# An AdaLN block on one core: FFN over pairs of steps, hidden weights read from DRAM, and a fixed plan of issue

## The chip, the cores and the metric

The kernel runs on one core of one Trainium2 chip. The metric is device time in microseconds (us) for one launch. The engines named are TensorE (matmuls; its weight loads are a row of their own in the profile), VectorE, ScalarE (ACT), GpSimd (POOL) and SyncE (SP), whose queue issues nearly all DMAs.

## The reference

An input x of 4 batches x 2048 tokens x 256 channels goes through a memory attention and then through an FFN, each behind a modulated layer norm. Cut to what is computed:

```python
h = layernorm(x) * (1 + ca) + sa          # ca, sa, ga, cb, sb, gb: per batch, from silu(c) @ wmod
x = x + ga * attn(h)
h = layernorm(x) * (1 + cb) + sb
x = x + gb * ffn(h)

# attn: 4 heads of 64, chunks of 64 tokens; rk = h / |h| per head, wk = rk shifted by one token, v = h @ Ww.T
A     = inv(eye - A0)                     # A0 = -(wk wk^T * decay), strictly lower, 64 x 64 per chunk and head
intra = strict(rk wk^T * decay)
def step(S, ...):                         # chunk after chunk
    v_new = A @ v - (A @ wk) @ S
    o     = rk_g @ S + intra @ v_new
    S     = gamma_C * S + wk_g @ v_new
attn = h + (alpha * o) @ Wr.T

# ffn: weights are -1, 0, 1 with a scale per output
h = silu(h @ w1) * (h @ w2)               # 256 -> 1024
h = gelu(h @ h1); h = gelu(h @ h2)        # 1024 -> 1024, erf form
ffn = h @ w3                              # 1024 -> 256
```

## The kernel before

*Steps.* A step is one chunk of 64 tokens of all four batches: 256 rows, held as 128 partitions x 2 halves. There are NS = 32 steps, and each has a local part (norms, keys, values, Gram matrices, the inverse), a recurrent part that needs the state S of the step before, and an FFN.

*Local part.* `local_norms` makes the modulated layer norm `hid` and the unit keys `rk`. `local_keys` transposes both on TensorE (`tp`) into `hT` and `keys`, `local_values` multiplies by Ww (`vp`), and `local_grams` makes the Gram matrices (`G`), masked by VectorE into `NMT` (for A) and `IT` (for intra). The diagonal 32 x 32 blocks go through DRAM (`d1`) into `U`, with one block a partition, 32 of them in four copies. `local_inverse` (L269, L271) inverts all of them by columns: 31 columns, two VectorE operations each, on `Z`. `local_blocks` brings them back over DRAM (`d2`) into `E`, `local_diagonal` transposes them, and `local_merge1` and `local_merge2` compute the off-diagonal blocks (`yp`, `ep`).

*Recurrent part.* `rec_state` multiplies S by the keys (`R`, `O`), `rec_values` multiplies by the inverse (`V`, then `vn`), `rec_update` makes the inner output and the new S (`new`, first the output, then the state), and `rec_out` multiplies by Wr (`ap_`, `ga`) and lets POOL add it to the step's `y` (L393).

*FFN.* `ffn_norm` normalises `y` into `xn`. `ffn_turn` transposes it (`tpf`), ACT applies the modulation in eight operations (`hm`), and `split` (L396 to L399) writes it as a high part, rounded to fp32r, and the low rest, so that two fp32r passes give the product. Eight tiles of `gated` (for w1 and w2, two products of 2 x 2 matmuls each), 16 of `hidden` (8 x 2 matmuls) and two of `last` (16 matmuls) follow. Their matmuls are at L462 in `product`. A tile's ACT or VectorE output is split as the next layer's input, by POOL in `gated` and by VectorE in `hidden`. A matmul of `gated` and `hidden` has 256 columns, the rows of one step. All five FFN weights stay in SBUF. A second branch, `steps(False)`, handles weights that fp32r can't hold; a flag from a comparison in the setup chooses, and with these inputs the first branch runs.

*Order.* `steps` interleaves by hand: while the FFN of step s runs, step s + 1 gets its merges and its recurrent part, step s + 2 its keys, Gram matrices and inverse, and step s + 3 its norms. Its core:

```python
f.gated(0) ... f.gated(7)             # local_keys(s + 2) after gated(1)
local_grams(s + 2); local_merge1(s + 1)
for q in range(16):
    # q 2 merge2, 3 rec_values, 5 rec_update, 7 rec_out, 8 local_values(s + 2),
    # q 9 ffn_norm, 11 ffn_turn(s + 1), 12 local_norms(s + 3)
    f.hidden(q // 8, q % 8)           # two columns of local_inverse(s + 2) after each from q = 3
rec_state(s + 2); f.last(0); f.last(1)
```

`tc.issue_after(x)` holds what is issued inside it behind instruction x; among what is free, a scheduler with a model of the times picks the order on each engine, and each engine then runs its instructions in that order. PSUM has three banks for FFN tiles (`pf`), two double ones for local work (`a2`) and one (`a1`). The local buffers `keys`, `v`, `rkg`, `hid` and `E` exist once, `rk`, `wkg`, `IT` and `NMT` twice, `y` four times.

Of the kernel before, what the change touches and what calls it, by code (L numbers as in the profile page):

```python
# [27 lines left out]
BF = mybir.dt.bfloat16  # L28
I32 = mybir.dt.int32
# [36 lines left out]

@with_exitstack
def adaln_block_kernel(ctx: ExitStack, tc: tile.TileContext, x_in, ww, wr, decay, log_alpha, w1, w2, h1, h2, w3, scol,
# [7 lines left out]
    N = B * C  # L76
    EPS = 1e-5

# [24 lines left out]
    fh1 = cp.tile([P, NH, HID], FR, name="fh1")  # L103
    fh2 = cp.tile([P, NH, HID], FR, name="fh2")
# [4 lines left out]
    ys = [cp.tile([P, 2, D], F32, name=f"y{n}") for n in range(4)]  # L109
    rks = [cp.tile([P, 2, D], F32, name=f"rk{n}") for n in range(2)]  # L110
    keys = cp.tile([P, 2, 2, 2, C + 1], F32, name="keys")
    v = cp.tile([P, 2, D], F32, name="v")
    rem = cp.tile([P, 2, D], F32, name="rem")
    rkg = cp.tile([P, 2, 2, 2, C], F32, name="rkg")
    hid = cp.tile([P, 2, D], F32, name="hid")
    wkgs = [cp.tile([P, 2, D], F32, name=f"wkg{n}") for n in range(2)]
    ITs = [cp.tile([P, 8, C], F32, name=f"IT{n}") for n in range(2)]
    NMTs = [cp.tile([P, 8, C], F32, name=f"NMT{n}") for n in range(2)]
    E = cp.tile([P, 8, C], F32, name="E")
    S = cp.tile([P, 2, 4, C], F32, name="S")  # L120
    U = cp.tile([P, K, K], F32, name="U")
    Z = cp.tile([P, 8, K], F32, name="Z")
    Dm = cp.tile([P, 8, K], F32, name="Dm")
    d1 = dp.tile([4, 8, K, K], F32, name="d1")
    d2 = dp.tile([K, 4, 8, K], F32, name="d2")

    nc.vector.memset(half, -0.5)
    nc.gpsimd.memset(keys, 0.0)
    nc.gpsimd.memset(S, 0.0)
    nc.gpsimd.memset(E, 0.0)  # L130
    nc.gpsimd.memset(wkgs[0], 0.0)
# [4 lines left out]
    mark = {}  # L136

    def after(name):

        return tc.issue_after(mark[name])  # L140

    def move(out, in_):
        mark["moved"] = nc.sync.dma_start(out=out, in_=in_).ins  # L143

    def flat(t):
        return t.rearrange("q n d -> q (n d)")
# [4 lines left out]
    def load(s):  # L151
        for b in range(2):
            move(out=ys[s % 4][C * b:C * b + C],
                              in_=x_in[b::2, s * C:(s + 1) * C, :].rearrange("q t d -> t q d"))

    def moments(x):

        mv = st.tile([P, 2, 2], F32, tag="mv", name="mv")
        for n in range(2):
            bs = st.tile([P, 6], F32, tag="bs", name="bs")  # L160
            nc.vector.bn_stats(bs, x[:, n, :])  # L161
            nc.vector.bn_aggr(mv[:, n, :], bs)
        rs = st.tile([P, 2], F32, tag="rs", name="rs")
        nc.vector.tensor_scalar(rs, mv[:, :, 1], EPS, None, ALU.add)  # L164
        nc.gpsimd.tensor_tensor(rs, rs, half[:, 0:2], ALU.pow)  # L165
        return mv, rs


    def local_norms(s):
        x, rk = ys[s % 4], rks[s % 2]  # L170
        mv, rs = moments(x)
        for n in range(2):
            nc.vector.scalar_tensor_tensor(hid[:, n, :], x[:, n, :], mv[:, n, 0:1], mod[:, CA, n, :],  # L173
                                           ALU.subtract, ALU.mult)
            nc.vector.scalar_tensor_tensor(hid[:, n, :], hid[:, n, :], rs[:, n:n + 1], mod[:, SA, n, :],  # L175
                                           ALU.mult, ALU.add)
        sq = ap.tile([P, 2, D], F32, tag="tmp", name="sq")
        nc.scalar.activation(sq, hid, AF.Square)
        rn = st.tile([P, 8], F32, tag="rn", name="rn")
        nc.vector.tensor_reduce(rn, heads(sq), AX.X, ALU.add)  # L180
        mark["norms"] = nc.vector.tensor_scalar(rn, rn, 1e-24, None, ALU.max).ins  # L181
        nc.gpsimd.tensor_tensor(rn, rn, half, ALU.pow)
        nc.gpsimd.tensor_tensor(heads(rk), heads(hid), over(rn, 2, C), ALU.mult)

    def local_residual(s, h=None):
        x, h = ys[s % 4], hid if h is None else h

        t = ap.tile([P, 2, D], F32, tag="tmp", name="gh")
        nc.gpsimd.tensor_tensor(t, h, mod[:, GA], ALU.mult)  # L189
        nc.gpsimd.tensor_tensor(x, x, t, ALU.add)  # L190

    def local_keys(s, first=False):
        rk = rks[s % 2]
        tp = ps2.tile([P, 2, 2, 2, P], F32, tag="a2", name="tp")
        for a, src in enumerate((hid, rk)):
            for p in range(2):
                for n in range(2):
                    nc.tensor.transpose(tp[:, a, p, n, :], src[:, n, p * P:(p + 1) * P], ident)  # L198
        hT = ap.tile([P, 2, 2, P], F32, tag="hT", name="hT")

        nc.scalar.copy(hT[:, :, 0, :], tp[:, 0, :, 0, :])
        nc.scalar.copy(hT[:, :, 1, :].rearrange("q p (b t) -> q p b t", t=C)[:, :, ::-1, :],
                       tp[:, 0, :, 1, :].rearrange("q p (b t) -> q p b t", t=C))
        k4 = keys.rearrange("q p n b t -> q (p n b) t")
        if s > 0:
            nc.vector.tensor_copy(k4[:, :, 0:1], k4[:, :, C:C + 1])
        nc.scalar.copy(k4[:, :, 1:C + 1], tp[:, 1].rearrange("q p n (b t) -> q (p n b) t", t=C))
        if not first:
            local_residual(s)
        return hT  # L210

    def local_reads():

        nc.gpsimd.tensor_tensor(rkg.rearrange("q p n b t -> q p (n b) t"),
                                keys.rearrange("q p n b t -> q p (n b) t")[:, :, :, 1:C + 1], over(gpT, 2, 4), ALU.mult)

    def local_writes(s):

        rk, wkg = rks[s % 2], wkgs[s % 2]
        for b in range(2):  # L220
            if s > 0:
                move(out=wkg[C * b:C * b + 1], in_=rks[(s - 1) % 2][C * b + C - 1:C * b + C])
            move(out=wkg[C * b + 1:C * b + C], in_=rk[C * b:C * b + C - 1])
        w4 = wkg.rearrange("q n (a d) -> q n a d", d=C)
        mark["keys"] = nc.gpsimd.tensor_tensor(w4, w4, over(over(gtail, 1, 2), 3, C), ALU.mult).ins  # L225

    def local_values(s, hT):
        vp = ps1.tile([P, 2, D], F32, tag="a1", name="vp")
        for n in range(2):
            for k in range(NK):  # L230
                nc.tensor.matmul(vp[:, n, :], lhsT=hT[:, k, n, :], rhs=wwT[:, k, :], start=k == 0, stop=k == NK - 1)  # L231
        nc.scalar.copy(v, vp)

    def local_keys_values(s):
        local_values(s, local_keys(s))

    def local_grams(s):
        IT, NMT = ITs[s % 2], NMTs[s % 2]

        G = ps2.tile([P, 2, 2, 256], F32, tag="a2", name="G")  # L240
        for p in range(2):
            for n in range(2):
                for h in range(2):
                    r = slice(C * h, C * h + C)
                    for b in range(2):
                        mark["grams"] = nc.tensor.matmul(G[C * b:C * b + C, h, p, n * (C + 1):(n + 1) * (C + 1)],
                                         lhsT=keys[r, p, n, b, 0:C], rhs=keys[r, p, n, b, :], start=True, stop=True).ins
        g4 = G.rearrange("q h p m -> q (h p) m")[:, :, 0:2 * (C + 1)].rearrange("q a (n t) -> q a n t", t=C + 1)
        nc.vector.tensor_tensor(NMT.rearrange("q (a n) t -> q a n t", n=2), g4[:, :, :, 0:C], over(NLT, 2, 2), ALU.mult)
        mark["masked"] = nc.vector.tensor_tensor(IT.rearrange("q (a n) t -> q a n t", n=2), g4[:, :, :, 1:C + 1], over(LT, 2, 2),  # L250
                                ALU.mult).ins
        for b in range(2):
            for k in range(2):
                r = slice(C * b + K * k, C * b + K * k + K)
                move(out=d1[2 * b + k].rearrange("u j i -> j u i"), in_=NMT[r, :, K * k:K * k + K])
        for g in range(4):
            move(out=U[K * g:K * g + K], in_=d1.rearrange("x u j i -> (x u) j i"))

        nc.gpsimd.memset(Z, 0.0)  # L259
        diag = Z.rearrange("q c i -> q (c i)")  # L260
        for g in range(4):
            nc.gpsimd.memset(diag[K * g:K * g + K, g::K + 4], 1.0)

    def local_inverse(s, j0, j1):

        for j in range(j0, j1):
            n, w = j // 4 + 1, K - 1 - j
            t = ap.tile([P, 8, K], F32, tag="zt", name="zt")
            nc.vector.tensor_tensor(t[:, 0:n, 0:w], Z[:, 0:n, j:j + 1].to_broadcast([P, n, w]),  # L269
                                    over(U[:, j, j + 1:K], 1, n), ALU.mult)  # L270
            mark["inverse"] = nc.vector.tensor_tensor(Z[:, 0:n, j + 1:K], Z[:, 0:n, j + 1:K], t[:, 0:n, 0:w],  # L271
                                                      ALU.add).ins

    def local_blocks(s):
        dst = d2.rearrange("(c g) x u i -> g (x u) c i", g=4)
        for g in range(4):
            move(out=dst[g], in_=Z[K * g:K * g + K])
        E4 = E.rearrange("q (a n) i -> q a n i", n=2)
        for b in range(2):
            for k in range(2):  # L280
                for n in range(2):
                    r = slice(C * (b ^ n) + K * k, C * (b ^ n) + K * k + K)
                    move(out=E4[r, :, n, K * k:K * k + K],
                         in_=d2[:, 2 * b + k].rearrange("j (a n) i -> j a n i", n=2)[:, :, n, :])

    def local_diagonal():

        E4, D4 = (t.rearrange("q (a n) i -> q a n i", n=2) for t in (E, Dm))
        nc.vector.transpose(D4[:, :, 0, :], E4[:, :, 0, 0:K])
# [515 lines left out]
```

## Time and profile before

| | us |
|---|---|
| median of 3 runs | 1799.43 (1796.76 to 1800.52) |
| profiled execution | 1796.47 |
| its span, first to last instruction | 1794.6 |
| first FFN matmul of step 0 | 96.7 |
| of step 1 | 167.9 |
| of step 2 | 229.07 |
| of step 31 | 1744.5 |
| last FFN matmul ends | 1788.4 |

The four starts are read from the timeline of TensorE. The profile gives, for each engine, its busy share of the span and how many instructions it ran; below it come rows of 40 slices (a digit is the busy share in tenths, PEclk the granted TensorE clock in tenths of full speed), and then groups of instructions as `out<-in` with their count, `busy, mean ns`, and the idle time before them with what ended most of it. Matmuls overlap in the pipe, so the distance between their starts, from the timeline, is the pace, and the mean of one is its latency. The timeline lists time, length, engine, instruction and count, with the idle time and its releaser in brackets. L numbers are lines of the kernel.

### The profile page before, as it was taken

How to read it: one execution, taken by the hardware profiler on the slowest of the kernel's cores; microseconds unless marked ns; L12 is line 12 of the kernel's file. 1: busy time of each engine (PE TensorE's matmuls, PEld its weight loads, DVE VectorE, ACT ScalarE, POOL GpSimd, SP SyncE). 2: the span in 40 equal slices, each digit the busy share in tenths (PEclk: the TensorE clock that was granted, in tenths of full speed). 3: DMA queues.
4: the chain of work that ended last, by engine and by line, in shares of the span. 5: the costliest groups of instructions: out<-in, count | busy, mean ns of one | idle time of the engine just before them, and what ended most of it. 6: DMA issues, size and time to landing. Idle time of an engine off the chain costs nothing.

```text
span 1794.6 us, 50335 instructions
## 1 busy us (share of the span) xinstructions
PE 1704.1 (95%) x20372; PEld 1623.5 (90%) x20372; DVE 1207.6 (67%) x3805; ACT 991.4 (55%) x2285; POOL 595.3 (33%) x742
## 2 busy tenths in 40 slices
PE   5478999999999999999999999999999999999998
PEld 3267999999999999999999999999999999999998
DVE  6876666677766667776666777666777766667532
ACT  5244555655555565555566555556555655665554
POOL 2232323342332334233234323323433333343111
PEclk8688999999999999999999999999999999999999
DMA  8220111111111110111111011111111111110100
GB/s 288 76 52 8 34 40 40 40 21 33 36 32 40 40 40 16 37 35 34 40 40 40 16 37 34 34 40 40 28 25 38 36 34 40 40 38 16 27 7 15
DMA packets 144659, 72.11 MB, mean 40 GB/s; under 512 B 114400, under 2 KB 132960, under 8 KB 144416
## 3 DMA queue, kind: packets, MB, share of 16 engines
q1 hardware_dynamic: 144416, 68.79, 15.6%
q8 instruction: 162, 2.65, 0.6%
q14 instruction: 81, 0.66, 0.1%
HBM read 43.57 MB, written 16.78 MB: 34 GB/s over the span
## 4 chain that ended last, share of the span: by engine, by line
DVE 47%; PE 29%; DMA 9%; POOL 4%; SPq 4%; issue 4%; ACT 2%; DVEq 0%; ACTq 0%; POOLq 0%
PE ps L462 24%; DVE zt L269 14%; DVE Z L271 11%; DVE act L399 6%; DMA out_dram<-y 4%; SPq L143 4%; DMA U<-d 4%; POOL act L399 3%; DVE bs L161 2%; DVE rn L181 2%; POOL y L501 1%; PE tp L198 1%; DVE hid L173 1%; DVE rn L180 1%; DVE hid L175 1%
## 5 line engine op out<-in xcount | busy, mean ns | idle before, releaser
L462 PE MATMUL ps<-act,fh 128*128 128x256 f32 x8192 | 1026.3, 283 | 1.2 <-DVE act L399 0.7
L462 PEld LDWEIGHTS ps<-act,fh 128*128 128x128 f32 x8192 | 981.9, 188 | 11.8 <-DVE act L399 1.2
L481 ACT ACTIVATE raw<-ps,sc 128x256 f32<-128x256 f32 x512 | 244.4, 479 | 407.6 <-PE ps L462 357.4
L269 DVE TENSOR_TENSOR zt<-Z,U 128x60 f32<-128x60 f32 (+24 forms) x992 | 291.7, 294 | 138.6 <-DMA U<-d 107.9
L399 DVE TENSOR_TENSOR act<-raw,act 128x256 fp32r<-128x256 f32 x512 | 213.2, 421 | 212.1 <-ACT act L398 211.9
L398 ACT CAST act<-raw 128x256 fp32r<-128x256 f32 x768 | 311.9, 407 | 39.6 <-DVE raw L473 23.1
L462 PE MATMUL ps<-hs,fw 128*128 128x256 f32 x2048 | 258.5, 283 | 15.6 <-DVE hs L399 6.7
L462 PEld LDWEIGHTS ps<-hs,fw 128*128 128x128 f32 x2048 | 247.9, 190 | 17.5 <-DVE hs L399 7.2
L271 DVE TENSOR_TENSOR Z<-Z,zt 128x60 f32<-128x60 f32 (+24 forms) x992 | 241.1, 243 | 22.2 <-DVE zt L269 0.5
L399 POOL TENSOR_TENSOR act<-raw,act 128x256 fp32r<-128x256 f32 x256 | 187.7, 739 | 148.0 <-ACT act L398 144.5
L393 POOL TENSOR_TENSOR y<-y,ga 128x512 f32<-128x512 f32 x32 | 41.3, 1291 | 503.1 <-DVE ga L392 478.6
L473 DVE SCALAR_TENSOR_TENSOR raw<-ps,sc,sg 128x256 f32<-128x256 f32 x256 | 123.5, 484 | 124.3 <-ACT sg L472 121.1
L472 ACT ACTIVATE sg<-ps,sc 128x256 f32<-128x256 f32 x256 | 122.0, 477 | 152.4 <-PE ps L462 144.0
L462 PE MATMUL ps<-fw,act 128*128 128x256 f32 x1024 | 138.4, 285 | 22.7 <-DVE act L399 22.0
L462 PEld LDWEIGHTS ps<-fw,act 128*128 128x128 f32 x1024 | 123.2, 188 | 33.2 <-DVE act L399 30.2
L165 POOL TENSOR_TENSOR rs<-rs,half 128x2 f32<-128x2 f32 x64 | 53.9, 842 | 132.3 <-DVE rs L164 132.3
L417 ACT ACTIVATE hm<-tpf,modT 128x64 f32<-128x64 f32 x256 | 82.3, 416 | 13.1 <-PE tpf L413 13.0
L231 PE MATMUL vp<-wwT,hT 128*128 128x256 f32 x256 | 63.8, 394 | 14.8 <-DVE modT L667 14.8
L189 POOL TENSOR_TENSOR gh<-hid,mod 128x512 f32<-128x512 f32 x32 | 50.8, 1586 | 75.4 <-DVE rn L180 75.3
L225 POOL TENSOR_TENSOR wkg<-wkg,gtail 128x512 f32<-128x512 f32 x32 | 33.4, 1042 | 115.9 <-DMA wkg<-rk 42.2
L231 PEld LDWEIGHTS vp<-wwT,hT 128*128 128x128 f32 x256 | 48.2, 198 | 21.0 <-ACT alc L645 15.2
L259 POOL MEMSET Z<- 128x256 f32 x32 | 10.1, 317 | 161.8 <-DMA d<-Z 161.8
(213 smaller groups left out, 1565.0 us busy)
## 6 DMA issues: line engine op xcount, KB each, us to landing
U<-d SPq DMA_DIRECT2D x128, 128.0 KB, 2.7
y<-in_x_dram SPq DMA_DIRECT2D x64, 128.0 KB, 2.9
st<-in_h_dram SPq DMA_DIRECT2D x16, 512.0 KB, 6.2
wkg<-rk SPq DMA_DIRECT2D x64, 126.0 KB
out_dram<-y SPq DMA_DIRECT2D x62, 128.0 KB, 2.5
d<-NMT SPq DMA_DIRECT2D x128, 32.0 KB, 1.6
d<-Z SPq DMA_DIRECT2D x128, 32.0 KB, 1.7
E<-d SPq DMA_DIRECT2D x256, 16.0 KB, 1.7
```

What stands on the lines that cost most here:

```text
L143: mark["moved"] = nc.sync.dma_start(out=out, in_=in_).ins
L165: nc.gpsimd.tensor_tensor(rs, rs, half[:, 0:2], ALU.pow)
L231: nc.tensor.matmul(vp[:, n, :], lhsT=hT[:, k, n, :], rhs=wwT[:, k, :], start=k == 0, stop=k == NK - 1)
L269: nc.vector.tensor_tensor(t[:, 0:n, 0:w], Z[:, 0:n, j:j + 1].to_broadcast([P, n, w]), over(U[:, j, j + 1:K], 1, n), ALU.mult)
L271: mark["inverse"] = nc.vector.tensor_tensor(Z[:, 0:n, j + 1:K], Z[:, 0:n, j + 1:K], t[:, 0:n, 0:w], ALU.add).ins
L398: nc.scalar.copy(to[0], a)
L399: return (eng or nc.vector).tensor_tensor(to[1], a, to[0].bitcast(F32), ALU.subtract).ins
L417: nc.scalar.activation(hm[:, k, b, :], tp[:, k, b // 2, C * (b % 2):C * (b % 2) + C], AF.Identity, bias=modT[:, k, b:b + 1], scale=modT[:, ...
L462: self.end = nc.tensor.matmul(ps, lhsT=wk if lhs_is_w else a, rhs=a if lhs_is_w else wk, start=k == 0 and i == 0, stop=k == k_n - 1 and i ...
L472: nc.scalar.activation(sg, ps[:, 0, :], AF.Silu, scale=sc[:, 0, o:o + 1])
L473: self.gate = nc.vector.scalar_tensor_tensor(to, ps[:, 1, :], sc[:, 1, o:o + 1], sg, ALU.mult, ALU.mult).ins
L481: nc.scalar.activation(to, ps[:, 0, :], AF.Gelu, scale=sc[:, 2 + layer, o:o + 1])
```

## The change

The FFN takes two steps at a time: steps 0 and 1 singly, then the 15 pairs 2g and 2g + 1. A matmul of `gated` and `hidden` then has up to 512 columns (N = 2 * B * C), the activations of a pair are one tile, and `last` still runs 128 rows a matmul, four times. In `gated` each of the two products has a PSUM bank of its own. POOL makes the low part for the first six gated tiles, VectorE for the last two.

The hidden weights no longer stay in SBUF. The setup writes h1 and h2 to DRAM, reordered so that what one output tile needs (512 KB) is contiguous, and each hidden tile reads its own into a ring of three. The setup's comparison with a rounded copy is replaced by a look at the low 16 bits of each weight. The SBUF that comes free holds second copies of `keys`, `v` and `rkg`, six `y`, and IT, E, Z, Dm for two steps; E takes the place of NMT and `rem` is gone.

The Gram matrices, the inverse and the merges are made for two steps at once: U holds 64 blocks twice instead of 32 blocks four times, one a partition, and Z 16 instead of 8 of their columns a partition. In `rec_update` the state's matmuls and the update of S come before the inner output.

The order of issue is a list. An FFN is cut into units (`yield`), 84 in a single FFN and 88 in a pair, and every local or recurrent function is put at a unit by `planned`; `stage` holds it behind the last instruction of every engine so far. `later` counts half as many units during the two single FFNs.

```diff
-    N = B * C
+    NP = NS // 2
+    N = 2 * B * C
+    def stage():
+        with ExitStack() as stack:
+            for e in engines:
+                if e.last is not None:
+                    stack.enter_context(tc.issue_after(e.last))
+            yield
...
-    fh1 = cp.tile([P, NH, HID], FR, name="fh1")
-    fh2 = cp.tile([P, NH, HID], FR, name="fh2")
+    fhs = [dp.tile([NH, P, NH, P], F32, name=f"fh{n}") for n in range(2)]
...
-    def local_inverse(s, j0, j1):
-        for j in range(j0, j1):
-            n, w = j // 4 + 1, K - 1 - j
+    def local_inverse(j):
+        n, w = j // 2 + 1, K - 1 - j
+        t = ap.tile([P, 16, K], F32, tag="zt", name="zt")
+        dve.tensor_tensor(t[:, 0:n, 0:w], Z[:, 0:n, j:j + 1].to_broadcast([P, n, w]), over(U[:, j, j + 1:K], 1, n),
+                          ALU.mult)
+        dve.tensor_tensor(Z[:, 0:n, j + 1:K], Z[:, 0:n, j + 1:K], t[:, 0:n, 0:w], ALU.add)
...
+        GATED, GELU, LAST = 16, 64, 8
+        UNITS = GATED + GELU + LAST
...
         def hidden(self, layer, o):
-            w, src = ((fh1, h1), (fh2, h2))[layer]
-            ps = pf.tile([P, 2, N], F32, tag="f", name="ps2")
-            self.product(ps[:, 0, :], self.weights(w, src, o * P, P))
+            ps = pf.tile([P, self.n], F32, tag="f", name="ps2")
+            if self.exact:
+                w = self.ring(NH)
+                move(out=w.bitcast(F32), in_=fhs[layer][o])
+            yield from self.product(ps, w, 4)
...
+        def layer(n):
+            to, w, k = parts[n]
+            move(out=to[:, :, k, :].rearrange("o p c -> p o c"), in_=staged[n].rearrange("q (o c) -> q o c", c=P))
...
+    FIRST = 2 * NU - Ffn.LAST
+        def recur(s, u):
+            add(u, rec_values, s, to="vn")
+            add(later(u, 3), rec_update, s, "=vn", "=oT", to="oT")
+            add(later(u, 6), rec_out, s, "=oT")
+            add(later(u, 10), ffn_norm, s, to="xn")
+            add(later(u, 13), turned, s)
+        def local(s, u, new=True):
+            if new:
+                add(u, local_hidden, s, hid, to="sq")
+                add(later(u, 3), local_sizes, "=sq", to="rn")
+                add(later(u, 4), local_units, s, hid, "=rn")
+                add(later(u, 9), local_residual, s, hid)
+            add(later(u, 7), local_shift, s)
+            add(later(u, 8), local_keys, s, hid, to="hT")
+            add(later(u, 11), local_values, s, "=hT")
+            add(later(u, 11), local_reads, s)
+            add(later(u, 12), local_writes, s)
...
+        for g in range(1, NP):
+            a, b = 2 * g, 2 * g + 1
+            if g > 1:
+                u = later(merge, 6)
+                add(max(u - 18, 0), load, a)
+                add(max(u + 2, 0), load, b)
+                local(a, u)
+                u = later(u, 11)
+            local(b, u)
+            add(later(u, 12), local_grams)
+            u = later(u, 21)
+            for j in range(K - 1):
+                add(later(u, j // 2 if g == 1 else j * 2 // 3), local_inverse, j)
+            u = later(u, K // 2 if g == 1 else (K - 2) * 2 // 3 + 1)
+            add(u, local_blocks)
+            merge = max(later(u, 11), FIRST + NU * (g - 2) + 10)
+            m = merge
+            add(m - 4, rec_state, a, to="oT")
+            add(m - 1, local_diagonal)
+            add(m, local_merge1, to="Y")
+            add(later(m, 3), local_merge2, "=Y")
+            recur(a, later(m, 6))
+            add(later(m, 12), rec_state, b, to="oT")
+            recur(b, later(m, 16))
...
+            for g, i in [(0, 0), (0, 1)] + [(g, None) for g in range(1, NP)]:
+                before, f = f, Ffn(g, i, had["hs"], fp, exact)
+                for n, _ in enumerate(f.run()):
...
+                    for what in plan.pop(u, ()):
+                        with stage():
+                            what()
+                    u += 1
```

## The prediction

> **What bounds the kernel now.** I read the page first: busy shares and the row of the granted TensorE clock, then the costliest groups.
>
> ```profile
> span 1794.6 us, 50335 instructions
> PE 1704.1 (95%) x20372; PEld 1623.5 (90%) x20372; DVE 1207.6 (67%) x3805; ACT 991.4 (55%) x2285; POOL 595.3 (33%) x742
> PEclk8688999999999999999999999999999999999999
> L462 PE MATMUL ps<-act,fh 128*128 128x256 f32 x8192 | 1026.3, 283 | 1.2 <-DVE act L399 0.7
> ```
>
> TensorE is full from slice 5 on, its clock is full there, and its 8192 hidden-layer matmuls lose 1.2 us to waits. The 283 ns is latency; what counts is the distance between starts. That is in the timeline of TensorE, over one step in the middle and then over the last step, which has no attention work beside it (columns: start, us, what, count, idle before):
>
> ```profile
> 882.39 0.69 PE L366 MATMUL new<-IT,vn 64*64 64x64 f32 x32
> 882.90 0.65 PE L369 MATMUL new<-vn,wkg 64*64 64x64 f32 x32
> 883.48 3.68 PE L462 MATMUL ps<-act,fh 128*128 128x256 f32 x29
> 887.00 1.89 PE L389 MATMUL ap__13449<-wrT,oT 128*128 128x256 f32 x8
> 888.54 3.53 PE L462 MATMUL ps<-act,fh 128*128 128x256 f32 x27
> 891.91 1.89 PE L231 MATMUL vp<-wwT,hT 128*128 128x256 f32 x8
> ...
> 898.00 0.60 PE L413 MATMUL tpf<-kept,xn 128*128 128x128 f32 x4
> 898.35 9.67 PE L462 MATMUL ps<-act,fh 128*128 128x256 f32 x80
> ...
> 911.12 0.50 PE L462 MATMUL ps<-fw,act 128*128 128x256 f32 x2 [0.33 <-DVE act L399]
> 912.39 2.21 PE L462 MATMUL ps<-fw,act 128*128 128x256 f32 x17 [0.77 <-DVE act L399]
> ```
>
> ```profile
> 1753.53 30.25 PE L462 MATMUL ps<-act,fh 128*128 128x256 f32 x256
> ```
>
> 256 matmuls in 30.25 us, less one latency of 0.28, is 0.1175 us a matmul of 256 columns. The local work of a step costs TensorE, start to next start in that timeline: `new` 1.09, `ap_` 1.54, `vp` 1.54, `tpf` 0.35, R and O 1.09, `tp` 0.79, G 0.63, `yp` 0.38, `ep` 0.62, V 0.63 (those not shown are in the same answer), together 8.66. The 352 FFN matmuls of a step are 41.1 at the mixed pace (256 x 0.1175, 64 gated at 0.113, 32 last at 0.117). Steps repeat every 52.3 us ((1744.5 - 229.07)/29 between the first FFN matmuls of step 2 and of step 31), so 2.5 us a step is waiting: 5.0 in a pair of 104.5.
>
> Where a turn of activations (`tpf`, then `hs`) is not covered, it looks like this, at the start of the second step:
>
> ```profile
> 163.48 0.49 PE L413 MATMUL tpf<-kept,xn 128*128 128x128 f32 x3
> ...
> 167.91 0.80 PE L462 MATMUL ps<-hs,fw 128*128 128x256 f32 x2 [3.82 <-ACT hs L398]
> 171.72 3.23 PE L462 MATMUL ps<-hs,fw 128*128 128x256 f32 x14 [3.02 <-DVE hs L399]
> ```
>
> In the steady steps `tpf` has 80 and more matmuls behind it (898.35), and the turn costs nothing. Last, what the groups say of the parts on other engines:
>
> ```profile
> L269 DVE TENSOR_TENSOR zt<-Z,U 128x31 f32<-128x31 f32 x32 | 6.1, 191 | 113.3 <-DMA U<-d 107.9 <-DMA E<-d 5.4
> L399 DVE TENSOR_TENSOR hs<-hm,hs 128x512 fp32r<-128x512 f32 x32 | 21.9, 684 | 2.4 <-ACT hs L398 2.4
> L398 ACT CAST hs<-hm 128x512 fp32r<-128x512 f32 x32 | 21.2, 661 | 0.1
> U<-d SPq DMA_DIRECT2D x128, 128.0 KB, 2.7
> ```
>
> The first column of the inverse holds VectorE 107.9 us in all (3.4 a step) until U has landed. It costs nothing now, since TensorE is then in the hidden layers.
>
> **What the Trainium skill says.** "TensorE: Matmul & The Clock Gate", Back-to-back issue gap: columns / 2.4 + 2.5 ns, so 109 ns at 256 and 216 at 512. The trace agrees at 512 columns' worth: `vp` takes (1.89 - 0.38)/7 = 0.216 us a pass. It disagrees at 256 (117.5). The section LDWEIGHTS gives columns / 1.2, 107 ns for 128, near the 117.5, and PEld is 90% busy: I read the pace at 256 as that of the weight load. Part 1 of the page lets the clock fall to half after some 3.4 us with little work; the PEclk row has 6 in the third slice, where TensorE had waits of 3 to 15 us. "SBUF — State Buffer", Who interferes with whom: a two-input VectorE operation locks out GpSimd or waits for it; the trace has `zt` of 28 columns at 1.04 us (909.25) beside the usual 0.2.
>
> **The change, part by part.**
>
> *Wider matmuls.* 320 gated and hidden matmuls a pair have 512 columns in place of 640 with 256; the 64 of `last` stay. Cost: 320 x 0.216 + 64 x 0.117 = 76.6 us a pair. Before: 82.2. The bounds are 0.216 (weight load hidden) and 0.235 (no gain, 82.7); I take 0.216 because `vp` with full weights shows it. Local TensorE work is the same, 17.3 a pair. Together 93.9.
>
> *Inverse of two steps at once.* One run of 31 columns for two steps. A pair of operations costs about 0.19 + 0.19 at 31 elements and 0.23 + 0.23 at 70; with up to 136 elements I estimate 0.25 each, 15.5 us against 2 x 31 x 0.41 = 25 now. Off the path: VectorE is at 67%. No credit. ACT and VectorE evictions of 512 columns (0.66 to 0.75 by the rows above, against 0.41 to 0.48) lie beside 3.5 us of matmuls a tile in the hidden layers: nothing.
>
> *Streamed hidden weights.* 16 x 512 KB a pair, one each 3.46 us (151 GB/s). The first slice moved 288 GB/s, and a 128 KB load lands in 2.7 us; at three buffers a slot has 7 us. In the built order of SyncE's queue the loads stand behind transfers that wait for the inverse and for E's blocks, but each has a tile to spare. I take 0; if that cover goes, about 2 us a pair.
>
> *The order of issue, which decides.* In the built order the inverse sits in the gated phase and the first hidden layer, the merges at the start of the second, both recurrences after that, and the second step's turn directly before the next pair's first matmul. Walking the four queues by hand with the durations above:
> 1. At the pair's border the chain runs `ap_`, `ga`, POOL's y, statistics, `xn`, `tpf`, with little FFN work left between. Waits: `tp` for `rk` 0.8 (POOL's two norm operations, 1.66 and 1.06, in front), `vp` for `hT` 0.65, `tpf` for `xn` 1.6.
> 2. After `tpf`, eight `hm` (2.45) and the cast (0.66) come before the first matmul, and G fills 1.26: 2.15 of waiting, then 0.25 for the low half. Items 1 and 2: 5.5.
> 3. Gated phase. VectorE has the masks of two steps and `gb` (5 x 0.68) ahead of the first gate; then the first inverse column stands between the third and the fourth gate and waits for U: masks, d writes, U's landing end 13 us after `tpf`. The fourth gate ends near 17.7, and a matmul needing its bank has waited 2.7. The order of ACT (two Silus, two casts) costs the rest. The phase takes 19.6 against 14.9 of work: 4.7.
> 4. Of the 5.0 waiting before I keep half, 2.5 (layer changes, the port lock, the clock after the border).
>
> Sum 12.7; a pair takes 106.6. Bounds of this sum: 7 (the gated phase costs 1, the chain at the border is 2 shorter, 1 of item 4) to 17 (half clock after each border, late weights).
>
> *Start.* Sixteen 512 KB writes of the reordered weights go out on SyncE's queue before the first blocks: 8.4 MB at 288 GB/s is 29 us after the 45 of loads, so the merges can begin at about 78, not 70.2: +8. Step 1's turn moves into the first FFN: -7 (the 3.82 and 3.02 above). Two single FFNs at 1.9 us a tile need 276 GB/s: +5. The border before the first pair: +5.5. The first two FFNs took 67 and 61 us against 52; of that excess I take 8 back. First pair at 229 + 3.5, say 232.
>
> *Sum.* 232 + 14 x 106.6 + last FFN 79.6 (76.6 and 3 waiting) + tail 6.2 (as now) = 1810 of span; the execution is 1.9 above its span (1796.5 to 1794.6), and the median shown 3.0 above that: 1815.
>
> **Rivals.**
> - *Faster (0.40): the wider matmuls carry.* Waits of 7.7 a pair: 101.6, so 232 + 1422 + 86 = 1740 and 1745 as a median. For: the walk adds every hop, and in the gated phase a shorter way to U removes most of item 3. Against: `tpf` and `hs` stand side by side, and the start of step 2 showed what that costs. It decides from 11.6 us of waiting a pair down; above, the kernel is slower.
> - *Much slower (0.12): the clock falls at every border, and weights come late.* The border leaves TensorE mostly idle for over 6 us. 110 a pair: 1863.
> - *The width gives nothing (0.04):* pace 0.235, 6.1 a pair more: about 1900.
> - *No difference (0.06):* 1796 to 1803; 0.2% is what this measurement can tell.
>
> **How the numbers follow.** The likeliest, slightly slower by the waits at the border and in the gated phase, has 0.38 and its own range 1803 to 1845. Slower in all is 0.38 + 0.12 + 0.04 = 0.54. The range of 1730 to 1863 leaves out the upper half of the last cases and the best fifth of the faster one.
>
> **What would show it.** `vp` and the 512-column matmuls at 0.216 apart: the first part right. A wait of `ps` for ACT's `hs` near 2 us once a pair: item 2. Waits of `ps` in the gated phase for VectorE with `zt` held by U: item 3. A PEclk row with eights would speak for the third case. I am wrong if the pair's period is 102 or less, or if the gated phase takes under 16 us.

## The result and the profile after

The change makes the kernel slower: 1958.62 us (median of 4 runs, 1957.06 to 1963.25) against 1799.68 for the kernel before, a ratio of 1.089 (95% interval 1.087 to 1.091). The prediction was 1815 with a range of 1730 to 1863. The page of the kernel after, profiled in an execution of 1957.66 us:

```profile
span 1955.8 us, 37975 instructions
PE 1731.8 (89%) x15572; PEld 1405.4 (72%) x15572; DVE 1023.3 (52%) x2426; ACT 813.8 (42%) x1467; POOL 509.2 (26%) x474
PEclk7679899999999999999899999999999898999999
```

TensorE has fallen from 95% to 89%, and its clock row, all nines from the fifth slice on before, has eights again and again. Nearly all instructions now show as L82, the line of a wrapper, so tiles identify them. The merges of one pair, then the border to the next, in the timeline of TensorE (start, us, what, count, idle time before and its releaser):

```profile
882.94 0.80 PE L82 MATMUL yp<-Dm,E 32*32 32x32 f32 x64
...
931.12 1.79 PE L82 MATMUL ps<-fw,act 128*128 128x256 f32 x12
932.74 0.60 PE L82 MATMUL tp<-kept,rk 128*128 128x128 f32 x4
933.80 1.99 PE L82 MATMUL vp<-wwT,hT 128*128 128x256 f32 x8 [0.46 <-ACT hT L82]
937.39 0.30 PE L82 MATMUL tpf<-kept,xn 128*128 128x128 f32 x1 [1.59 <-DVE xn L82]
938.64 0.76 PE L82 MATMUL tpf<-kept,xn 128*128 128x128 f32 x3 [0.95 <-DVE xn L82]
939.33 2.01 PE L82 MATMUL G<-keys 64*64 64x65 f32 x64
942.63 8.34 PE L82 MATMUL ps<-hs,fw 128*128 128x512 f32 x28 [1.28 <-ACT hs L82]
...
957.47 2.83 PE L82 MATMUL ps<-hs,fw 128*128 128x512 f32 x8 [2.42 <-DVE raw L82]
960.57 4.95 PE L82 MATMUL ps<-hs,fw 128*128 128x512 f32 x16 [0.27 <-DVE raw L82]
965.62 11.22 PE L82 MATMUL ps<-act,w 128*128 128x512 f32 x48
978.75 2.87 PE L82 MATMUL ps<-act,w 128*128 128x512 f32 x8 [1.92 <-DMA w<-fh]
```

These are the places that the prediction walked: `xn`, `hs`, then the gates (`raw`) behind the inverse. The last of these is seen on VectorE, where the first column of the inverse stands between the third gate (950.18) and the fourth (956.67) and waits for U:

```profile
953.85 0.19 DVE L82 TENSOR_TENSOR zt<-Z,U 128x31 f32<-128x31 f32 x1 [2.92 <-DMA U<-d]
```

But 28 matmuls take 8.34 us at 942.63, where 28 at 0.227 (the pace at 965.62, (11.22 - 0.43)/47 = 0.230, hardly differs) take 6.8. The table of stretches says why (stretch, length, busy time of TensorE, weight loads, VectorE, ACT and POOL, granted clock, DMA share, GB/s):

```profile
940.00:945.00 5.00, 3.72 (x58) 3.00 (x51) 2.40 (x4) 3.82 (x9) 2.58 (x5) 0.50 0.00 0
945.00:950.00 5.00, 5.00 (x21) 3.76 (x20) 2.73 (x5) 2.95 (x5) 1.57 (x2) 0.93 0.53 99
950.00:955.00 5.00, 5.00 (x81) 3.63 (x79) 1.80 (x6) 1.83 (x4) 2.27 (x2) 1.00 0.73 167
```

The waits of TensorE over 14 pairs (263.4 to 1863.5; total, times, longest):

```profile
PE ps L82 <- DVE raw L82: 40.7, 33, 2.8
PE tpf L82 <- DVE xn L82: 28.5, 25, 1.6
PE ps L82 <- ACT hs L82: 26.8, 13, 2.1
PE ps L82 <- DMA w<-fh: 20.2, 12, 3.1
```

With the smaller ones it is 126.5 us, 9.0 a pair; in the kernel before the same list over 28 steps had one entry of 20.6. Of the 161 us between the two spans, 34 lie ahead of the first pair (it starts at 263.4; step 2 started at 229.1), 130 in 14 pairs of 114.3, and the end gives 3 back (92.3 from the last pair's start, against 95.1 from the start of step 30). The same 28 steps took 105.0 us for two before (step 30 starts at 1699.45); the 104.5 of the prediction also counts step 30, which has less local work beside it and took 44.5 us.

### The profile page after: what moved, and what is told of

Read it like the earlier page. It is cut to its first block, busy times and chain, and to the rows that moved or that the text cites. A ratio compares the mean times of both kernels' runs of the same rounds, so it can differ in the third digit from the quotient of the medians.

```text
span 1955.8 us, 37975 instructions
## 1 busy us (share of the span) xinstructions
PE 1731.8 (89%) x15572; PEld 1405.4 (72%) x15572; DVE 1023.3 (52%) x2426; ACT 813.8 (42%) x1467; POOL 509.2 (26%) x474
## 4 chain that ended last, share of the span: by engine, by line
PE 56%; DVE 14%; DMA 9%; ACT 6%; POOL 4%; SPq 3%; issue 2%; DVEq 0%; POOLq 0%; ACTq 0%
PE ps L82 47%; ACT hm L82 4%; DMA w<-fh 3%; SPq L82 3%; DMA U<-d 3%; DVE Z L82 2%; DVE zt L82 2%; DVE raw L82 2%; DVE xn L82 2%; DMA wkg<-rk 1%; PE vp L82 1%; POOL rn L82 1%; PE new L82 1%; DVE E L82 1%; PE V L82 1%
## 5 line engine op out<-in xcount | busy, mean ns | idle before, releaser
L82 PE MATMUL ps<-act,w 128*128 128x512 f32 (+1 forms) x4352 | 992.2, 384 | 39.3 <-DMA w<-fh 25.9
L82 PEld LDWEIGHTS ps<-act,w 128*128 128x128 f32 x4352 | 780.6, 190 | 202.2 <-ACT act L82 16.7
L82 DVE TENSOR_TENSOR act<-raw,act 128x512 fp32r<-128x512 f32 (+1 forms) x306 | 204.4, 670 | 454.8 <-ACT act L82 436.0
L82 ACT ACTIVATE raw<-ps,sc 128x512 f32<-128x512 f32 (+1 forms) x272 | 178.8, 664 | 448.8 <-PE ps L82 424.3
L82 PE MATMUL ps<-hs,fw 128*128 128x512 f32 (+1 forms) x1088 | 299.0, 432 | 67.7 <-ACT hs L82 33.3
L82 PEld LDWEIGHTS ps<-hs,fw 128*128 128x128 f32 x1088 | 217.6, 214 | 138.9 <-DVE raw L82 44.3
L82 ACT CAST act<-raw 128x512 fp32r<-128x512 f32 (+1 forms) x408 | 240.6, 595 | 129.7 <-DVE raw L82 122.3
L82 POOL TENSOR_TENSOR rn<-rn,half 128x8 f32<-128x8 f32 x32 | 52.6, 1644 | 718.6 <-DVE rn L82 718.6
L82 POOL TENSOR_TENSOR act<-raw,act 128x512 fp32r<-128x512 f32 (+1 forms) x102 | 125.3, 1235 | 249.9 <-ACT act L82 249.9
L82 DVE TENSOR_TENSOR zt<-Z,U 128x126 f32<-128x126 f32 (+22 forms) x496 | 147.8, 298 | 44.7 <-DMA U<-d 32.1
L82 DVE TENSOR_TENSOR Z<-Z,zt 128x126 f32<-128x126 f32 (+22 forms) x496 | 156.2, 315 | 13.5
L82 PE MATMUL ps<-fw,act 128*128 128x256 f32 x1024 | 133.2, 285 | 2.1 <-DVE gb L82 2.0
L82 PEld LDWEIGHTS ps<-fw,act 128*128 128x128 f32 x1024 | 126.5, 189 | 4.6 <-DVE gb L82 2.2
L82 DVE SCALAR_TENSOR_TENSOR raw<-ps,sc,sg 128x512 f32<-128x512 f32 (+1 forms) x136 | 97.1, 715 | 55.2 <-PE ps L82 30.2
L82 ACT ACTIVATE sg<-ps,sc 128x512 f32<-128x512 f32 (+1 forms) x136 | 90.1, 662 | 82.8 <-PE ps L82 82.0
L82 POOL TENSOR_TENSOR rs<-rs,half 128x2 f32<-128x2 f32 x64 | 53.7, 839 | 208.4 <-DVE rs L82 194.1
L82 ACT ACTIVATE hm<-tpf,modT 128x64 f32<-128x64 f32 x256 | 79.4, 417 | 62.6 <-PE tpf L82 62.6
L82 POOL TENSOR_TENSOR y<-y,ga 128x512 f32<-128x512 f32 x32 | 41.2, 1287 | 149.7 <-DVE ga L82 142.5
L82 DVE TENSOR_TENSOR hs<-hm,hs 128x512 fp32r<-128x512 f32 x32 | 26.0, 814 | 101.1 <-ACT hs L82 101.0
L82 PE MATMUL vp<-wwT,hT 128*128 128x256 f32 x256 | 65.1, 390 | 6.6 <-ACT hT L82 5.5
L82 DVE BATCH_NORM_STATS2 bs<-y 128x6 f32<-128x256 f32 x128 | 48.8, 417 | 37.9 <-POOL y L82 31.1
```

What stands on the lines that cost most here:

```text
L82: made = make(*args, **kwargs)
```

## Experiments

Edits are on the changed kernel unless another is named. Most are shown as a short diff, cut to what matters; the others are told in the expectation.

**Is the order of issue at fault?** The plan puts a pair's merges at unit 10 and the second step's turn at unit 39 of the FFN before it, well ahead of the border (unit 88). In the trace the merges run 40 units later (882.94, behind 135 of the pair's hidden matmuls) and the turn almost 50 (937.39, behind the last matmul). The code explains it: `stage` holds the local work behind the FFN, nothing holds the FFN behind the local work.

```diff
 made = make(*args, **kwargs)
+if self.tc is not None:
+    self.tc.keep_in_program_order(made)   # in the steps, every engine
```

> Edit: every instruction of the steps is also held behind the one written before it on its engine, FFN included; nothing else. Theory 1 (the order slips: only the local work is held behind the FFN, not the FFN behind the local work, so the local work runs about 40 units after its place in the plan, and the border waits, the waits of the gated phase and the drops of the clock all come from that): the turn of the second step lies in the middle of the hidden layers, no wait of ps for ACT's hs once a pair, a period of about 101 us (98.5 of matmuls at the measured 0.230 us for 512 columns, plus 2 to 3 of waiting) in place of 114.3, and about 1770 us (1750 to 1790). Theory 2 (the streamed weights and their queue are what holds TensorE): waits for w stay or grow, the period stays above 108, over 1880 us. Theory 3 (the recurrence is too slow a chain for this plan wherever it stands): waits of PE for VectorE and ACT inside the hidden layers take the place of those at the border, over 1850 us.

Measured: 2522.71 us. My expectation failed by a wide margin; the waits show that the place of the turn isn't all (waits of TensorE in the whole run):

```profile
PE ps L82 <- DMA w<-fh: 508.9, 61, 16.6
```

And SyncE's queue in one pair, where nothing was issued from 1144.4 to 1159.8:

```profile
1159.79 1.93 SPq L82 DMA_DIRECT2D d<-E  x4
1163.20 1.15 SPq L82 DMA_DIRECT2D U<-d  x2
1164.45 23.64 SPq L82 DMA_DIRECT2D w<-fh  x7
```

A tile's weights are asked for where the tile is written; in a fixed order they stand behind `d` and `U`, which wait for VectorE's masks. The scheduler of the changed kernel had moved them ahead. With this edit on top,

```diff
-                w = self.ring(NH)
-                move(out=w.bitcast(F32), in_=fhs[layer][o])
+                w = self.still[(8 * layer + o) % 3]   # three tiles, loaded once
```

> Edit on top of the kept order: the hidden weights are not streamed; three tiles are loaded once and used for all hidden tiles, so that the hidden layers multiply by the wrong weights. Theory 2 (streaming costs much by late weights or by contention in SBUF): 30 us or more below the kept order, and the pace at 512 columns falls from 0.230 toward 0.216. Theory 1: the weights are hidden once the order is kept, less than 10 us below it (the waits for w were 1.7 us a pair), and the pace stays at 0.230.

1989.82 us, 533 less: in that order the loads are the loss. What is left, 116 us a pair, has two waits of 3.9 us for `oT`, which VectorE does behind an `act` that waits for ACT. So a fixed order is not good in itself.

The start's queue, on top of `kept` and then on the changed kernel alone (the second layer's weight writes behind `local_blocks`):

> Edit on top of the kept order: in the setup, the eight 512 KB writes of the second hidden layer's weights go out behind the transfers of the first inverse instead of ahead of them. If SyncE's queue is what held the first merges (they start at 98.6 us after the change, the transfers of Z being issued at 89.4 behind the writes): merges near 87, and 9 to 13 us less than the kept order alone. If not (the inverse itself was late): no difference, within 3 us.

> Edit to the changed kernel alone: in the setup the eight 512 KB writes of the second hidden layer's weights go out behind the transfers of the first inverse. On the fully kept order this edit gave 8 us less, inside the interval. If SyncE's queue is what makes the first merges late: they start near 87 us in place of 98.6, and the whole is 8 to 14 us less than 1958.6. If the inverse or its input is late anyway: within 4 us.

2514.97 us (its interval overlaps that of `kept`) and 1965.70, so no gain. In the second, the merges start at 92.1 us, not 87, and the first FFN 6.3 us earlier than after the change (116.75). Of that, 2.5 us are left at the first pair (260.9), and the pairs take 115.1; why wasn't looked into. In the kernel after, the queue read

```profile
61.13 26.46 SPq L82 DMA_DIRECT2D fh<-st  x16
89.35 2.07 SPq L82 DMA_DIRECT2D d<-Z  x2
```

and with `early` d is written at 84.3, when the inverse ends. So the writes cost 5 us there. The rest of the late start is not the length of the first inverse, but when it can begin. The first column, in the kernel before and after:

```profile
38.84 0.17 DVE L269 TENSOR_TENSOR zt<-Z,U 128x31 f32<-128x31 f32 x1
64.36 1.01 DVE L82 TENSOR_TENSOR zt<-Z,U 128x31 f32<-128x31 f32 x1
```

The inverse of two steps takes 19.9 us (to 84.2), that of one took 17.6 (to 56.5). But it waits for the masks of both steps: `d` is first written at 39.4 in place of 28.6, and from there to the first column pass 25.0 us in place of 10.2. DMA was full in the first part of that stretch (387 GB/s from 38 to 48).

**The pace, measured by itself.**

> Not the block at all: groups of 128 matmuls with 128x128 weights, alone on the chip and then beside VectorE, ACT or 512 KB loads. If the pace of fp32r is its own: 0.228 to 0.231 us at 512 columns and 0.117 at 256 with nothing beside it, bf16 0.216 and 0.109, and little change with weights that stay the same. If the weight load sets the 256-column pace, as the prediction had it: the same 0.117 for bf16 at 256, and 0.216 for fp32r at 512. If traffic on SBUF makes the difference: 0.216 alone, 0.230 beside the others.

The timeline of TensorE, each line 128 matmuls (256 and 512 columns under `same`, alone; 256 of bf16 under `b`; 512 under `dma`, beside loads that move 294 GB/s from 239 to 247 us; 512 under `all`):

```profile
87.03 15.52 PE L94 MATMUL same<-af,wf 128*128 128x256 f32 x128
102.38 29.20 PE L94 MATMUL same<-af,wf 128*128 128x512 f32 x128
131.42 14.15 PE L94 MATMUL b<-ab,wb 128*128 128x256 bf16 x128
231.09 29.18 PE L94 MATMUL dma<-af,wf 128*128 128x512 f32 x128
260.10 29.18 PE L94 MATMUL all<-af,wf 128*128 128x512 f32 x128
```

512 columns of fp32r: (131.42 - 102.38)/128 = 0.227 us alone and (260.10 - 231.09)/128 = 0.227 beside the loads. 256 columns: (102.38 - 87.03)/128 = 0.120. bf16 takes 0.109, and at 512 columns most of its starts are 0.216 apart. So the pace is fp32r's own: some 11 ns a matmul more than bf16 at either width, and traffic doesn't make it. A weight load that only bounds the pace at 256 columns would not show at 512. The weight loads differ too (190 ns for fp32r, 99 for bf16 in this run), but those of `vp` in the kernel before last as long (198 ns in the mean), and its passes start 0.216 apart, so their length alone isn't the cause. What the 11 ns are stays open.

**TensorE's order alone, then with room in it.**

```diff
-            e.last, e.tc = None, tc      # as in kept
+            e.last = None
+        pe.tc = tc
```

> Edit: only TensorE's instructions are held in the order in which the program writes them; VectorE, ACT, POOL and SyncE stay with the scheduler. In the fully kept order the loads of w stood behind SyncE's transfers for d, U and E (waits of up to 16.6 us); in its version without streaming two waits of 3.9 us for oT a pair came from VectorE's and ACT's fixed order. Theory 1 (what the change loses is the late place of the local work on TensorE: border, inverse beside the gates, half clock after them): with the turn in the middle of the hidden layers and the loads free, a period of 100 to 106 us in place of 114.3 and 1770 to 1850 us. Theory 2 (streaming cannot be hidden beside the transfers of the inverse in any order): waits for w over 8 us a pair, period over 112, over 1930 us.

1941.61 us, 113.2 a pair: less gained than expected. The waits for `w` are nearly gone (3.6 us in all); a wait of 4.3 us for `oT` stands in 12 of the 14 pairs, and work at half the clock follows it (`ap_` took 1.89 before):

```profile
904.24 3.75 PE L82 MATMUL ap__9290<-wrT,oT 128*128 128x256 f32 x8 [4.28 <-DVE oT L82]
```

```diff
+            more = (0, 0, 0) if s < 4 else (2, 2, 4)   # on rec_out, ffn_norm, turned
-            recur(b, later(m, 16))
+            recur(b, later(m, 16 if g == 1 else 19))   # and rec_state of b at 15
```

> Edit on top of the one before: from pair 2 on, two units more between the update of S and the output product, two more between that and its norm, four more before the turn, and the second step's recurrence three units later. If the waits that are left on TensorE are those for oT and xn (a chain that is too short for its latency): 3 to 6 us a pair less than the one before, 1740 to 1800 us. If they are waits for w or for the inverse: no difference beyond 1%.

1863.33 us, 95 below the change, 78 below `kept_pe`. A pair takes 107.4 us in the mean of the 14, 5.8 less, inside the 3 to 6 expected; the total is above the range of 1740 to 1800, which didn't follow from it (1941.6 less 14 x 6 is 1858). Its border:

```profile
920.96 1.99 PE L82 MATMUL ps<-fw,act 128*128 128x256 f32 x15
923.28 6.09 PE L82 MATMUL ps<-fw,act 128*128 128x256 f32 x49 [0.34 <-DVE act L82]
929.22 6.69 PE L82 MATMUL ps<-hs,fw 128*128 128x512 f32 x28
...
997.64 0.60 PE L82 MATMUL tpf<-kept,xn 128*128 128x128 f32 x4
997.99 4.92 PE L82 MATMUL ps<-act,w 128*128 128x512 f32 x19
```

`ps` of the next pair follows `last` without a wait, since `tpf` ran with over 130 hidden matmuls behind it; 28 matmuls take 6.69 us, not 8.34. The merges run 44 matmuls into the gated phase (941.60), which is the planned place.

**Is the room enough without the hold?** The same spacing with TensorE's order left to the scheduler:

> Edit to the changed kernel alone: the wider spacing of the recurrence from pair 2 on, as in pe_wide, with TensorE's order left to the scheduler. If what pe_wide gained comes from the hold (without it the local work slips to the end of the pair whatever the plan says): a border with waits for xn and hs, a period of 112 us or more and 1930 to 1975 us. If the spacing alone does it: a period near 106 and 1860 to 1890 us.

1946.33 us, 113.4 a pair, as expected if the hold is needed. The waits at the border are back (in the whole run):

```profile
PE ps L82 <- DVE raw L82: 36.6, 28, 2.2
PE ps L82 <- DMA w<-fh: 26.4, 19, 3.3
PE ps L82 <- DVE hs L82: 16.6, 13, 1.8
```

The hold alone gave 17 us, the spacing alone 12, both 95: the plan has to be kept, and it has to be one that can be kept.

**What width and streaming are worth there**, both on `pe_wide`, with TensorE's order unchanged. Width: two matmuls of 256 columns for each of 512.

```diff
-                pe.matmul(ps, lhsT=w[:, k, :], rhs=self.a[:, k, i, :], ...)
+                pe.matmul(ps[:, at_], lhsT=w[:, k, :], rhs=self.a[:, k, i, at_], ...)   # twice
```

> Edit on top of pe_wide, with TensorE's order held as it is there: each 512-column matmul of the gated and hidden layers is two of 256 columns, so that only the width is undone. If width is worth what the prediction took (0.216 against 0.235, 320 matmuls a pair): 6.1 us a pair or 90 us more than pe_wide's 1863. If it is worth what the trace of the change and the pace measured alone say (0.227 to 0.230 against 0.235 to 0.240): 1.6 to 4.2 us a pair, 24 to 63 us more.

1938.43 us, 75 more, between the two estimates; 112.5 us a pair, 5.0 more. The pace explains at most 320 x (0.240 - 0.227) = 4.2. A wait of 1.5 us a pair (`ps` for ACT's `act`) came in, and the mean granted clock over the 14 pairs fell from 0.99 to 0.98, so the 5.0 are not the width alone. Its hidden layers and those of the kernel before, in the last FFN:

```profile
1892.19 29.06 PE L82 MATMUL ps<-act,w 128*128 128x256 f32 x240 [0.34 <-DVE act L82]
```

(29.06 - 0.28)/239 = 0.120; before it was 0.1175. The width, with the waits that came with its loss, is worth 5.0 us a pair against this kernel at 256 columns and, by pace, at most 2.1 against the kernel before (82.2 less 320 x 0.227 and 7.5 for `last`). With the paces seen inside the block (0.230 at 965.62 after the change, 0.233 at 929.22 in `pe_wide`) it is about 1. Why 256 columns took 2.5 ns less there wasn't tried.

> Edit on top of pe_wide: the hidden weights are not streamed, three tiles loaded once serve all hidden tiles (wrong weights in the hidden layers). In pe_wide the waits for w add up to 3.4 us. If streaming costs only its waits: within 8 us of 1863. If 512 KB every 3.5 us also slows TensorE, VectorE or the small transfers of d, U and E: 20 us or more below.

1860.94 us, 2.4 less: in this order the loads cost next to nothing.

**What is left.**

> Edit on top of pe_wide: from pair 2 on the keys two units later (behind POOL's rk, which held tp 1.8 us a pair), the transposes of the diagonal blocks two units earlier (yp waited 1.1 us a pair for Dm), and in the setup the second layer's weights written behind the first inverse. If these waits are what is left to gain: 2 to 3 us a pair and 6 us at the start, 1815 to 1835 us, still above the kernel before. If they only move to the next dependence: 1850 or more.

1897.43 us: worse. With the keys, the edit starts the second step's norm one unit later and the Gram matrices and the inverse three. On ACT the copy `vn` now stands behind the square of that norm (`sq`), which waits for VectorE's `hid`, and TensorE waits for `vn`:

```profile
992.43 0.63 ACT L82 ACTIVATE sq<-hid 128x512 f32<-128x512 f32 x1 [2.23 <-DVE hid L82]
992.97 0.57 ACT L82 COPY vn<-V 128x512 f32<-128x512 f32 x1
993.59 1.13 PE L82 MATMUL new<-vn,wkg 64*64 64x64 f32 x32 [3.86 <-ACT vn L82]
994.49 1.08 PE L82 MATMUL new<-IT,vn 64*64 64x64 f32 x32
```

After 3.86 us of idling `new` takes 1.13 instead of 0.69. The wait comes in 13 of the pairs, 45.4 us in all. The expectation below puts it down to `vp`; in the trace `vp`'s copy follows `vn`. Without the move of the keys and what went with it:

> Edit on top of pe_wide, two of the three edits of pe_best: the transposes of the diagonal blocks two units earlier and the second layer's weights written behind the first inverse, the keys where pe_wide has them. In pe_best yp no longer waited for Dm, but the keys' move put vp beside V and a wait of 3.9 us for vn came. If the keys alone did that: 0.9 us a pair and 6 us at the start less than pe_wide, 1838 to 1850 us. If the earlier transposes cost VectorE as much elsewhere: 1860 us or more.

1830.00 us (ratio 1.018, interval 1.015 to 1.021), the best of these and below what was expected (the two edits weren't told apart: the first pair starts 8.2 us earlier than in `pe_wide`, and a pair takes 2.0 less); 105.4 us a pair, 104.5 once it is steady (595.6 to 1640.2), with no half clock between the second pair and the end. Two steps of the kernel before took 104.9 over about the same stretch (599.1 to 1648.1). Its span is 30.1 us longer: the later start costs 30.6 (259.7 against 229.1), and the first two pairs, in which the merges wait 5.2 and 9.0 us for the inverse's blocks (`Dm`), take 114.9 and 116.6, together 19 more than the same steps before; the 12 pairs after them win 13 back, and the end 6.5:

```profile
405.44 1.47 PE L82 MATMUL yp<-Dm,E 32*32 32x32 f32 x64 [9.01 <-DVE Dm L82]
```

So where the wide order runs steadily it is a little faster than the old one, and what it lacks lies in the setup and the first two pairs. A better order there wasn't tried, and no version here beats the kernel before.

## Why the prediction was wrong

- *Sign and mechanism*: slower, by waits at the border and in the gated phase, was right, but 8.9%, not 0.9%. The pairs took 114.3 us, not 106.6 (108 of the 146 us of span missed), the first pair began at 263.4, not 232 (31), and the end took 92.3, not 85.8 (6). The 7.7 us a pair are 3.5 of work, 2.8 of clock and 2.6 in item 4, less 1.2 in the waits.
- *Wider matmuls, the first step that failed*: I took 0.216 because `vp` shows it. `vp` isn't fp32r. Measured, 0.227: 320 x 0.011 = 3.5 us a pair. I had read the pace at 256 columns as that of the weight load, after the 107 ns that the Trainium skill's "TensorE: Matmul & The Clock Gate", LDWEIGHTS, gives for 128 columns; that reading fell with the pace kernel, where the same 11 ns stand at 512. The width's gain over the kernel before shrinks from 5.6 to at most 2.1 us a pair.
- *Waits, items 1 to 3*: 10.2 predicted at border and gates; 4.5 recorded at the border (`xn`, `hT`, `hs`; 5.5 predicted) and 2.9 at the gates (`raw`; 4.7 predicted). The places were right. With the weights (1.4) and the rest it is 9.0. The gated phase still took 23.0 us in the pair shown (942.63 to 965.62), not 19.6: work at half the clock falls into it.
- *Item 4* was too small: what no recorded wait explains is 5.1 us a pair (114.3 less 97.4 of matmuls at measured paces, 9.0 and the 2.8 below), against 2.5. Part of it is the pace inside the block (0.230 to 0.233, as above, not 0.227); the rest was not traced. The 5.0 that it starts from was 5.5, by the 105.0 us above.
- *The clock, put into a rival with 0.12*: it falls at every border from the second pair on. Over the 14 pairs the mean granted clock is 0.97 (1.00 before), and some 200 matmuls start 0.43 us apart instead of 0.227: 40 us, 2.8 a pair. The same page's "Part 1: The HAM clock gate" speaks of a free-running window of some 3.4 us; the trace agrees, the half clock comes in stretches of 3.4 or 6.8 us. It fell at 938.8 after three waits that add up to 3.0 us (933 to 939), so no single long wait was needed. I had priced the border's waits and read its consequence as a separate case. (The 6 in the clock row before is in its second slice, not its third.)
- *Streamed weights at nothing*: nearly right; 1.4 us of waits a pair (2 if the cover went), and 2.4 us in all in `wide_still`. The cover is the scheduler's: in the fixed order the same loads cost 509 us of waiting.
- *Inverse off the path*: right where the order is kept (`pe_wide`, 0.3 us a pair for `raw`), wrong beside the gates, as item 3 said.
- *Start*: the writes were to cost 8 us at the first merges, which came at 98.6, not 78. The writes cost 5. What the prediction put at nothing is that the first inverse now waits for two steps' masks and their transfers: it begins 25.5 us later.
- *The rival "faster"* needed under 11.6 us of waiting. In the steady pairs of the trimmed order all that isn't matmuls at measured paces is 7.1 (104.5 less 97.4), inside the 7.7 that it allowed. The pair is still only 0.4 us below the old one, since its work was taken 3.5 us too low.

## What to carry to other kernels

A hold binds one side: local work that is queued behind the main loop can still slip (here by 40 to 50 of 88 units) if nothing queues the loop behind it, so look where it runs in the trace, not where the plan puts it. Take a pace from an operation of the same type and from the same kernel's form, since a few ns in each of thousands of matmuls decide a change that lives on width. A wait of TensorE costs more than its length where the clock falls after it, as it did here. And ask of every part that is made for two steps at once when its inputs are all there: the first one starts later, even if it takes no longer.

## What was not expected of the hardware

fp32r costs about 11 ns a matmul more than bf16, at 256 columns (0.120 against 0.109) as at 512 (0.227 against 0.216), with nothing else running and, at 512, beside loads of 294 GB/s. One idle stretch of 3.9 us was followed by work at about half the pace (`new` 1.13 against 0.69 us in `pe_best`, `ap_` 3.75 against 1.89 in `kept`).
